# Raw weight loads of a two-layer cross-attention kernel: from SyncE's DMA queue to ScalarE's, and a different lead for the attention steps

## The chip, the cores and the metric

The kernel runs on one core of a Trainium2 chip. A core has five engines that run side by side, each through its own instructions in order: TensorE (PE; its weight loads are listed as PEld), VectorE (DVE), ScalarE (ACT), GpSimd (POOL) and SyncE (SP). Engines wait for each other by semaphores. SP computes nothing here; it issues DMA transfers. The metric is the time of one execution on the device in microseconds (us), smaller is better.

## The reference

Two cross-attention layers run one after the other on `x` (8 batches of 100 rows, 512 wide) with a context `ctx` (8 batches of 722 rows). All is float32.

```python
# layer 0: 16 heads of 32
qn, kn, vn = layer_norm(x), layer_norm(ctx), layer_norm(ctx)
Q, K, V = qn @ wq + bq, kn @ wk + bk, vn @ wv + bv
x1 = x + softmax(Q K^T / sqrt(32)) V @ wo + bo
x2 = x1 + gelu(layer_norm(x1) @ w1 + b1) @ w2 + b2     # 512 -> 2048 -> 512
# layer 1: 8 + 8 heads of 64, no biases
out = softmax((x2 @ Wq) (ctx @ Wk)^T / 8 - 2) (ctx @ Wv) @ Wfc + x2
out = layer_norm(out) * gamma + beta
```

## The kernel before, in words

**Numbers.** Each float32 operand of a matmul is held as two float16 parts, a high and a low one, and most products are three matmuls (`TERMS`: high x high, high x low, low x high). So weights must be scaled and split before use, and this work on the weights is what the change touches.

**Units and heads.** The work is 24 units (`unit_of`): units 0 to 7 are the batches of layer 0, with 16 heads each; units 8 to 23 are the two halves of each batch of layer 1, with 8 heads each. `step(u, h)` (L1465) is the attention of one head: `scores` makes S (PE) and the row maximum `nm` (DVE, 901 ns); in layer 0 `negated` and `negated_T` bring the maximum back into the queries through a small matmul into `nzb` and a copy to `QS` (ACT), and one or two heads later `front0` makes the transposed scores ST (PE), the exponential `p` (ACT), its high part `pt` (ACT) and its low part (POOL). In layer 1 `front1` makes `p` from S, splits it into a `stage` tile (DVE or ACT, then POOL), and a transposing DMA issued by SP fills `pt`. `head_back` multiplies `pt` by V into O (PE). Between the steps, the main loop at the end of the function places pieces of the other work: projections of K and V for the next unit (`pp` and sometimes `nzb` are their PSUM tiles; their results `KN` go through DRAM (`KD`) or directly to `ks`), normalised and transposed context (`prep0`, `prep1`: `nat`, `hl`, `ctxT`), queries (`QN`, `QD`, `QS`), output projections, the feed-forward part (`ffn`, weights by `wst`), and the preparation of weights.

**Preparation of weights.** Layer 0's wq, wk, wv and wo are loaded at the start (`load0`, SP), and are not part of the change. The others (w1, w2, Wq, Wk, Wv, Wfc) are 32 blocks of 512 KB each (`block`, L1057). A block has four stages. `load` (L1061) takes the next of three ring tiles `STG` (named `stage` in the trace, L81) and issues one DMA. `norm` (L1073) squares the block on ACT with a running sum (`hl<-stage`). `scale` adds the sum over partitions with a small matmul (into O or `pp`) and finds a power of two on DVE. `piece` (two for each block) scales and splits half of the block: the high part on ACT (`whl<-stage` or `wres<-stage`), the low part on DVE for one piece, and for the other by an ACT copy (`stage<-stage`) and a subtract on POOL. The result goes to DRAM, from where `wst` tiles fetch it later, or to resident tiles `wres`. The three `stage` tiles are first used for the first context rows, at the start, then by the blocks, and in layer 1 by the attention. `pipeline` (L1045) orders the stages so that loads run ahead of the pieces, as far as three tiles allow.

**What sets the order.** The kernel is written in one program order, and a scheduler then fixes one order of instructions for each engine before the launch. It takes instructions that its model holds to be ready, by their place in the program. Two things bend that. `with tc.high_priority(offset=n)` counts the instructions inside as if they stood n places earlier; `step` uses 105 (80 near the last unit). And `nc.in_order` (L34 to L43, L49) names engines whose instructions keep program order among themselves; `block`'s `load` sets it to `("sync",)` around its DMA, so on SP this load keeps its place among the other loads and start-up transfers that are held so, while an instruction of an engine that isn't named is not held. At the start (L1270 to L1376) almost everything is held in a written order; after that the scheduler is free but for these loads.

Every instruction is recorded by the helper `call` at L40, so the trace gives L40 for all of them; groups are told apart by their tiles.

Of the kernel before, what the change touches and what calls it, by code (L numbers as in the profile page):

```python
# [54 lines left out]
def xattn_kernel(  # L55
# [4 lines left out]
    nc = Core(tc)  # L60
# [49 lines left out]
    def ring(name, tiles):  # L110
        i = counters.get(name, 0)
        counters[name] = i + 1
        return tiles[i % len(tiles)]
# [28 lines left out]
    def small(n=1, dt=F32, tag="sm"):  # L142
        return pool.tile([128, n], dt, tag=f"{tag}{n}", name=f"{tag}{n}", bufs=4)
# [12 lines left out]
    def pow2(*args):  # L156
        for f in pow2_steps(*args):
            f()
# [53 lines left out]
    def colsum(src, n, p=128):  # L212

        ps = psum_misc()
        nc.tensor.matmul(out=ps[:, :n], lhsT=ones[:p, :], rhs=src, start=True, stop=True)
        return ps[:, :n]
# [116 lines left out]
    def split_piece(dst_hi, dst_lo, raw, s, on_pool=False):  # L333
        nc.scalar.activation(dst_hi, raw, AF.Copy, scale=s)
        if on_pool:
            nc.scalar.activation(raw, raw, AF.Copy, scale=s)
            nc.gpsimd.tensor_tensor(dst_lo, raw, dst_hi, ALU.subtract)
            return
        nc.vector.scalar_tensor_tensor(dst_lo, raw, s, dst_hi, ALU.mult, ALU.subtract)
# [30 lines left out]
    def hlt():  # L370
        return ring("hl", HL)
# [324 lines left out]
    def scores(u, h):  # L696
        L, b, hf = unit_of(u)
        S = ps_s.tile([128, 2, 512], F32, tag="S", name="S")
        KS, q = KSt[u, h // 4], QSt[u]
        for j in range(2):  # L700
            sl = slice(j * HALF, (j + 1) * HALF)
            if L == 0:
                nc.tensor.matmul(
                    out=S[:SQ, j, :HALF], lhsT=q[:96, h, :], rhs=KS[:96, h % 4, sl], start=True, stop=True)
            else:
                for t in range(2):
                    nc.tensor.matmul(
                        out=S[:SQ, j, :HALF], lhsT=q[:, t, h, :], rhs=KS[:, h % 4, sl], start=(t == 0), stop=(t == 1))
        nm = small(1, tag="nm")
        nc.vector.tensor_reduce(nm[:SQ], S[:SQ, :, :HALF], AX.XY, ALU.max, negate=True)  # L710
        return S, nm
# [3 lines left out]
    def negated(nm):  # L715
        nz = ring("nm", NM)
        nc.vector.tensor_scalar(nz[:, 96:97], nm[:SQ], 1.0 / MS, None, ALU.mult)
        nc.vector.tensor_scalar(nz[:, 97:98], nz[:, 96:97], -MS, nm[:SQ], ALU.mult, ALU.add)
        return nz

    def negated_T(u, h, nz):
        q = QSt[u]
        z = NZB[:98, h % 4 * 128 : h % 4 * 128 + SQ]
        nc.tensor.matmul(out=z, lhsT=nz, rhs=ident16[:SQ, :SQ], start=True, stop=True)
        nc.scalar.copy(q[96:98, h, :], z[96:98])

    def front0(u, h, nz):
        KS, q = KSt[u, h // 4], QSt[u]
        T = ps_s.tile([128, 2, 512], F32, tag="S", name="ST")
        for c in range(NCH):  # L730
            nc.tensor.matmul(
                out=T[:, c // 3, (c % 3) * SQ : (c % 3) * SQ + SQ], lhsT=KS[:98, h % 4, c * 128 : c * 128 + 128],
                rhs=q[:98, h, :], start=True, stop=True)
        P = ring("p32", P32)[:, : 6 * SQ].rearrange("p (c q) -> p c q", q=SQ)
        nc.scalar.activation(
            P.rearrange("p (a c) q -> p a (c q)", a=2), T[:, :, : 3 * SQ], AF.Exp, scale=sig0)
        pt = ring("pt", PT)
        nc.scalar.copy(pt[:, 0:6, :SQ], P)
        for c in range(0, 6, 3):
            nc.gpsimd.tensor_tensor(  # L740
                pt[:, 6 + c : 6 + c + 3, :SQ], P[:, c : c + 3], pt[:, c : c + 3, :SQ], ALU.subtract)
        return pt

    def front1(u, h, S, nm):
        L, b, hf = unit_of(u)
        if h == 0:
            sums[u] = pool.tile([128, 8], F32, tag="sums", name="sums", bufs=3)
        sg = sig1[:SQ, 2 * hf + h // 4, b : b + 1]
        nb = small(1, tag="nb")
        nc.vector.tensor_tensor(nb[:SQ], nm[:SQ], sg, ALU.mult)  # L750
        P = ring("p32", P32)[:SQ]
        nc.scalar.activation(
            P.rearrange("p (a k) -> p a k", a=2), S[:SQ, :, :HALF], AF.Exp, bias=nb[:SQ], scale=sg,
            accum_out=sums[u][:SQ, h : h + 1])
        p16 = ring("p16", P16)
        if h % 2 == 0:
            nc.vector.tensor_copy(p16[:SQ, 0, :SK], P)
        else:
            nc.scalar.copy(p16[:SQ, 0, :SK], P)
        eng = nc.vector if u == LAST and h >= 4 else nc.gpsimd  # L760
        eng.tensor_tensor(p16[:SQ, 1, :SK], P, p16[:SQ, 0, :SK], ALU.subtract)
        pt = ring("pt", PT)
        nc.sync.dma_start_transpose(pt[:, :, 0:SQP], p16.rearrange("p t k -> p (t k)"))
        return pt
# [69 lines left out]
    LAST = 3 * B - 1  # L834
# [222 lines left out]
    def block(w, kind, i, col, scr=None, dst=None, total=None, done=None):  # L1057

        st = {}

        def load():  # L1061
            raw = ring("raw", STG)
            if kind == "rows":
                st["raw"] = raw.rearrange("p (c n) -> p c n", c=2)
                src = w[i * 256 : (i + 1) * 256, :]
            else:
                st["raw"] = raw.rearrange("p (c n) -> p c n", c=KC)
                src = w[:, i * 256 : (i + 1) * 256]
            nc.in_order = ("sync",)
            nc.sync.dma_start(out=st["raw"], in_=src.rearrange("(c p) n -> p c n", p=128))  # L1070
            nc.in_order = ()

        def norm():  # L1073
            st["u"] = u = small(1, tag="ub")
            nc.scalar.activation(
                hlt(), st["raw"].rearrange("p c n -> p (c n)"), AF.Square, accum_out=u)

        def scale():
            ut = colsum(st["u"], 1)
            t = small(1, tag="ut") if total is None else total[:, i : i + 1]  # L1080
            nc.vector.tensor_copy(t, ut)
            ut = t
            pow2(SC[:, 0, col : col + 1], SC[:, 1, col : col + 1], ut, 7, 1)
            if done is not None:
                done()

        def piece(k):
            raw, s = st["raw"], SC[:, 0, col : col + 1]
            counters["pc"] = counters.get("pc", 0) + 1
            op = counters["pc"] % 2 == 0  # L1090
            half = raw[:, k, :] if kind == "rows" else raw[:, :, k * 128 : (k + 1) * 128]
            if dst is not None:
                w1res[dst] = WRES[dst]
                at = i % 2 * 256 + k * 128
                split_piece(WRES[dst][:, 0, :, at : at + 128], WRES[dst][:, 1, :, at : at + 128], half, s, op)
                return
            o = more.tile([128, 1024], F16, tag="whl", name="whl", bufs=2)
            if kind == "rows":
                split_piece(o[:, :E], o[:, E:], half, s, op)
                nc.sync.dma_start(out=scr[2 * i + k].rearrange("p a b -> p (a b)"), in_=o)  # L1100
            else:
                v = o.rearrange("p (c t n) -> p c t n", c=KC, t=2)
                split_piece(v[:, :, 0, :], v[:, :, 1, :], half, s, op)
                nc.sync.dma_start(out=scr[2 * i + k].rearrange("p a b c -> p (a b c)"), in_=o)
        return dict(load=[(0.1, load)], norm=[(0.8, norm)],
                    scale=[(0.4, scale)], pieces=[(0.8, lambda k=k: piece(k)) for k in range(2)])

# [355 lines left out]
    pending = []  # L1463

    def step(u=None, h=None):  # L1465

        with tc.high_priority(offset=80 if u == LAST or u is None and len(pending) and pending[0][0] >= LAST - 1 else 105):
            new = None
            if u is not None:
                S, nm = scores(u, h)  # L1470
                new = (u, h, S, negated(nm) if u < B else nm)
                if u < B:
                    negated_T(u, h, new[3])
            if len(stages) >= (2 if u is not None and u < B else 1):
                v, g, S_, nm_ = stages.pop(0)
                pending.append((v, g, front0(v, g, nm_) if v < B else front1(v, g, S_, nm_)))
                used.add((v, g))
            if new:
                stages.append(new)
# [84 lines left out]
```

## Time and profile before

| what | value |
|---|---|
| runs shown (median, lowest, highest) | 1545.39, 1542.56, 1549.36 us |
| profiled execution | 1544.16 us |
| its span, first to last instruction | 1542.4 us |
| mean granted TensorE clock | 0.967 |
| DMA moved | 279.20 MB, mean 181 GB/s |
| SP's issues of the 32 blocks | 16 of w1 and w2 from 164.5 to 327.2 us, the last at 616.9 us |
| DMAs issued by ACT | 4, in the first 3 us, 450 to 528 ns each |

How to read it: the page gives each engine's busy time and its share of the span. A line of the waits names the waiting engine and the tile that it was to work on, then who ended the wait, then the total in us, the number of waits and the longest. A line of a group of instructions gives engine, operation, written tile <- read tiles and the count. The granted clock is TensorE's share of its full speed. All later numbers of the profile are from the one profiled execution.

### The profile page before, as it was taken

Reading aid. Unit: us, or ns where it says so; the run is one execution under the profiler, and the core shown is the slowest. Engines: PE = TensorE matmul, PEld = TensorE weight load, DVE = VectorE, ACT = ScalarE, POOL = GpSimd, SP = SyncE. Lnnn points to the kernel's source line nnn. Section 1 sums busy time; section 2 is a strip of 40 time slices with the busy share of each in tenths; the row PEclk is TensorE's granted clock in tenths of the full one; section 3 lists DMA queues with packets and bytes.
Section 4 is the critical chain, followed back from the end, with each engine's and each line's share of the span. In section 5 each row is a group of like instructions: output and inputs, shape, how many; then the busy total and the mean of one; then the engine's idle time right before and its main releaser. Section 6 shows DMA issues by size and latency. Waiting matters only on the chain.

```text
span 1542.4 us, 33741 instructions
## 1 busy us (share of the span) xinstructions
PE 1386.5 (90%) x12586; PEld 983.2 (64%) x12586; DVE 1019.0 (66%) x2761; ACT 813.9 (53%) x1550; POOL 578.1 (37%) x570
## 2 busy tenths in 40 slices
PE   6888888887879999888999899999899999999996
PEld 5666676665657776556666566576566676566674
DVE  7878778879795776575455755456755555646555
ACT  4456667787865776554344343444344544334442
POOL 3245466655564453462122321322322322313341
PEclk9899889999989999999999999999999999999998
DMA  8567898897976556569576879767869868866684
GB/s 218 127 144 191 213 259 219 228 229 200 251 148 179 164 190 194 122 155 205 140 179 188 170 174 213 170 159 192 179 155 217 189 159 192 186 157 159 148 170 110
DMA packets 456636, 279.20 MB, mean 181 GB/s; under 512 B 348932, under 2 KB 387860, under 8 KB 456472
## 3 DMA queue, kind: packets, MB, share of 16 engines
q1 hardware_dynamic: 454328, 277.02, 73.8%
q8 instruction: 99, 1.62, 0.5%
q14 instruction: 65, 0.53, 0.1%
q10 hardware_dynamic: 2112, 0.01, 0.1%
q0 software_dynamic: 32, 0.01, 0.0%
HBM read 150.88 MB, written 35.30 MB: 121 GB/s over the span
## 4 chain that ended last, share of the span: by engine, by line
PE 45%; DMA 12%; DVE 5%; SPq 5%; ACT 3%; issue 3%; POOL 1%; POOLq 0%; ACTq 0%; DVEq 0%
PE pp L40 27%; PE nzb L40 10%; SPq L40 5%; PE S L40 4%; PE O L40 4%; DMA pt<-stage 2%; DMA xs<-X 2%; DMA ks<-KN 2%; DVE nm L40 1%; ACT p L40 1%; DMA stage<-in_L_xattn_Wk_dram 1%; DMA QS<-QD 1%; DMA wst<-WFS 1%; DMA wst<-W1S 1%; DMA ctxT<-hl 1%
## 5 line engine op out<-in xcount | busy, mean ns | idle before, releaser
L40 POOL TENSOR_TENSOR stage<-p,stage 100x722 f16<-100x722 f32 x124 | 194.4, 1572 | 484.2 <-DVE stage L40 254.2
L40 PE MATMUL pp<-ctxT,wres 128*128 128x361 f16 x1836 | 326.8, 327 | 22.4 <-DVE KN L40 5.6
L40 PE MATMUL pp<-wres,ctxT 128*128 128x256 f16 (+3 forms) x2004 | 337.3, 320 | 8.0 <-DVE nm L40 3.0
L40 PEld LDWEIGHTS <-wres 128*128 128x128 f16 x2496 | 241.8, 101 | 151.4 <-issue 32.9
L40 PEld LDWEIGHTS <-ctxT 128*128 128x128 f16 (+1 forms) x2376 | 238.0, 104 | 140.8 <-issue 14.5
L40 DVE TENSOR_REDUCE nm<-S 100x1 f32<-100x722 f32 x256 | 230.0, 901 | 69.1 <-PE S L40 63.7
L40 POOL TENSOR_TENSOR pt<-p,pt 128x300 f16<-128x300 f32 x256 | 200.5, 806 | 178.5 <-ACT pt L40 105.0
L40 PE MATMUL O<-V,pt 128*128 128x64 f16 (+5 forms) x3840 | 200.3, 191 | 19.0 <-DMA pt<-stage 6.5
L40 PEld LDWEIGHTS <-pt 128*128 128x128 f16 (+1 forms) x3840 | 173.1, 99 | 57.4 <-DMA pt<-stage 8.1
L40 PE MATMUL S<-ks,QS 128*100 128x361 f16 (+1 forms) x768 | 175.7, 326 | 29.2 <-DVE nm L40 8.8
L40 ACT ACTIVATE p<-S,nb,sig 100x722 f32<-100x722 f32 x128 | 121.7, 952 | 120.8 <-DVE nb L40 104.3
L40 DVE TENSOR_TENSOR V<-pp,V 128x256 f16<-128x256 f32 (+2 forms) x196 | 90.7, 464 | 108.5 <-ACT V L40 107.9
L40 ACT CAST V<-pp 128x256 f16<-128x256 f32 (+2 forms) x196 | 79.1, 407 | 150.0 <-PE pp L40 105.1
L40 PEld LDWEIGHTS <-QS 128*100 128x100 f16 (+1 forms) x768 | 87.5, 127 | 54.5 <-issue 25.5
L40 ACT ACTIVATE p<-ST,sig 128x600 f32<-128x600 f32 x128 | 97.1, 759 | 27.3 <-PE ST L40 21.2
L40 PEld LDWEIGHTS <-wst 128*128 128x128 f16 x1152 | 99.8, 98 | 13.8 <-issue 4.0
L40 ACT CAST KN<-pp 128x361 f16<-128x361 f32 x89 | 40.9, 460 | 98.0 <-PE pp L40 91.9
L40 ACT CAST pt<-p 128x600 f16<-128x600 f32 x128 | 87.9, 690 | 2.1
L40 PE MATMUL nzb<-ctxT,wres 128*128 128x361 f16 x468 | 82.9, 321 | 2.4 <-DVE sx L40 1.3
L40 DVE TENSOR_TENSOR KN<-pp,KN 128x361 f16<-128x361 f32 x89 | 47.2, 531 | 53.3 <-ACT KN L40 51.6
L40 PE MATMUL nzb<-wres,ctxT 128*128 128x512 f16 (+2 forms) x372 | 80.4, 365 | 0.0
L40 PE MATMUL ST<-QS,ks 98*128 98x100 f16 x768 | 60.0, 210 | 16.5 <-ACT p L40 12.4
(268 smaller groups left out, 2038.7 us busy)
## 6 DMA issues: line engine op xcount, KB each, us to landing
ks<-KN SPq DMA_DIRECT2D x256, 90.2 KB
nat<-in_ctx_dram SPq DMA_DIRECT2D x78, 256.0 KB
ks<-KD SPq DMA_DIRECT2D x96, 180.5 KB
wst<-W1S SPq DMA_DIRECT2D x64, 256.0 KB
wst<-W2S SPq DMA_DIRECT2D x64, 256.0 KB
wst<-WFS SPq DMA_DIRECT2D x48, 256.0 KB
KD<-KN SPq DMA_DIRECT2D x32, 361.0 KB
QS<-QD SPq DMA_DIRECT2D x85, 100.0 KB
```

Source lines behind the costliest of these rows:

```text
L40: r = f(*args, **kwargs)
```

## The change

The DMA of a block's `load` is called on `nc.scalar` instead of `nc.sync`: ACT issues it, in ACT's own DMA queue. `nc.in_order` still names `sync` alone around it, so the load isn't held in program order any more. And the lead of `step` becomes 120 instead of 105; the 80 near the last unit stays.

```diff
             nc.in_order = ("sync",)
-            nc.sync.dma_start(out=st["raw"], in_=src.rearrange("(c p) n -> p c n", p=128))
+            nc.scalar.dma_start(out=st["raw"], in_=src.rearrange("(c p) n -> p c n", p=128))
             nc.in_order = ()
...
-        with tc.high_priority(offset=80 if u == LAST or u is None and len(pending) and pending[0][0] >= LAST - 1 else 105):
+        with tc.high_priority(offset=80 if u == LAST or u is None and len(pending) and pending[0][0] >= LAST - 1 else 120):
```

## The prediction

> **What bounds the kernel now.** I first read the page's busy times and its rows of DMA, then a table of busy time by stage, then what TensorE (PE) waits for, and last the lines of the loads that move.
>
> From the page:
>
> ```profile
> PE 1386.5 (90%) x12586; PEld 983.2 (64%) x12586; DVE 1019.0 (66%) x2761; ACT 813.9 (53%) x1550; POOL 578.1 (37%) x570
> ...
> q1 hardware_dynamic: 454328, 277.02, 73.8%
> ...
> HBM read 150.88 MB, written 35.30 MB: 121 GB/s over the span
> ```
>
> PE is busy for 90% of the span, so a change off PE can win back at most the other 155.9 us. Nearly all data goes through q1, SyncE's queue. By stage (columns: span, busy PE, PEld, DVE, ACT, POOL, then granted clock, DMA share, GB/s):
>
> ```profile
> 160.00:460.00 300.00, 247.76 (x2598) 191.70 (x2596) 249.86 (x812) 225.81 (x419) 173.39 (x198) 0.92 0.87 220
> 460.00:700.00 240.00, 216.36 (x2171) 159.13 (x2170) 157.35 (x415) 151.67 (x278) 114.09 (x128) 0.96 0.60 166
> 700.00:1500.00 800.00, 766.07 (x6427) 509.98 (x6425) 458.82 (x1038) 342.88 (x682) 218.20 (x151) 0.99 0.76 176
> ```
>
> All 32 loads that change lie between 164.5 and 617 us. There PE idles 52.2 + 23.6 us; after 700 us it idles 34 us in 800. In the first row the granted clock is 0.92, which is 24 us of full clock lost in 300; beside 52.2 us idle that is 0.46 us for each idle one. Where PE idles less (third row) the clock is 0.99. I therefore count one us of PE waiting in layer 0 as **1.46 us**. The dips come with idleness, but the trace doesn't show which wait makes which dip, so the factor lies between 1 and about 1.5.
>
> What PE waited for between 160 and 700 us (total, times, longest):
>
> ```profile
> PE ST L40 <- ACT p L40: 11.9, 11, 1.9
> PE pp L40 <- DVE KN L40: 9.2, 9, 3.6
> PE nzb L40 <- ACT QS L40: 7.5, 10, 1.6
> PE S L40 <- DVE nm L40: 5.4, 5, 1.8
> PE O L40 <- ACT hl L40: 4.4, 2, 3.7
> PE nzb L40 <- DVE nm L40: 3.4, 3, 2.0
> PE pp L40 <- DVE nm L40: 3.4, 3, 1.9
> PE S L40 <- ACT p L40: 3.3, 6, 1.6
> PE S L40 <- DMA QS<-QD: 3.2, 1, 3.2
> ```
>
> The attention chain (score, maximum, QS, ST, exp) ends most of it. Transfers end 9.1 us (QS 3.2, yT 2.3, pt 1.4, WOS 1.1, WQS 0.8, ks 0.3). A raw load acts through the block's square on ACT (the row PE O <- ACT hl). The loads on SyncE (min/median/max ns), and who waited for them (us, times):
>
> ```profile
> L40 SPq DMA_DIRECT2D stage<-in_L_xattn_w_dram x16: 383/396/507, 164.5 to 327.2; - x16
> ...
>   ACT hl L40: 12.7, 10
> ```
>
> The worst of those waits, on ACT, in front of the first blocks:
>
> ```profile
> 168.93 1.06 ACT L40 ACTIVATE hl<-stage 128x1024 f16<-128x1024 f32 x1 [2.60 <-DMA stage<-in_L_xattn_w_dram]
> ...
> 172.22 1.06 ACT L40 ACTIVATE hl<-stage 128x1024 f16<-128x1024 f32 x1 [0.65 <-DMA stage<-in_L_xattn_w_dram]
> ```
>
> **The change, part by part.** I compared the orders of the two built programs. The first three loads move from head 21 of layer 0 to ACT's setup, right behind the last readers of the three ring tiles (about 31 us). The other 29 stay within a head or a few of where they were, since a load can't start before the pieces of the block three earlier are done. Negative is a gain; times are PE waiting unless said otherwise.
>
> 1. SyncE loses 32 issues. Their durations sum to 13.4 us of some 260 us that it issues between 160 and 700 us: 5%. What waits behind them are ks, QS, wst and the transposes, whose waits on PE are the 9.1 us above. 5% of 9.1 is **-0.5**. Bounds: -9.1 (all gone) and 0, since the queue loses work and gains none.
>
> 2. The first three loads are early. ACT no longer idles 2.60 + 0.65 us at 169 to 172 us; PE's own gaps behind it there are 0.78, 0.33, 0.31 and 1.17 us on the timeline: **-2.6**. Bounds -4.4 (the whole row PE O <- ACT hl) and 0. If this cover goes, POOL and the attention chain are late next.
>
> 3. Those three loads, 1.57 MB, now run at 31 to 40 us, beside the transposes of ctxT and xT that SyncE issues from 31.5 to 37.7 us; PE waits 3.5 us for ctxT there, on the path. The DMA share is 0.61 and 0.64 in 30 to 40 us and 0.20 in 40 to 45. At 272 GB/s (10 to 20 us) the loads are 5.8 us of all engines, and 30 to 50 us leaves some 9.8 us free, so most is hidden: **+1.5**. Bounds 0 and +8.7 (all of it in front, at the mean 181 GB/s).
>
> 4. ACT gains 32 issues. Three fall into ACT's idle gaps of 1.28 and 1.79 us at 31 and 35 us. The other 29 at 0.42 us are 12.2 us on an engine that runs in order; queued behind each are p, QS, pt and V, which PE waits for. PE's waits for ACT (11.9, 7.5, 4.4, 3.3 and smaller ones, 29.3 us) beside ACT's 377.5 busy us are 0.078 us for each ACT us: **+0.95**. Bounds 0 (all in ACT's idle quarter) and +12.2.
>
> 5. ACT now does the loads' waits. Each load waits for POOL's subtract of the last piece. In the trace it ends 1.2 to 3.2 us, mean 1.6, after the end of ACT's own part of that piece. In the built order the load stands mostly 4 to 7 ACT instructions behind; the fifth instruction started 2.8 us behind in the mean, so only 0.7 us of waiting would have come in 32 blocks. Four stand 2 or 3 behind and may wait about 1 us. In 27 of 32 the load also waits on a DMA semaphore, that of an earlier transfer out of eight in turn; the spacing of SyncE's issues (425 in 540 us, 1.27 us) puts that some 10 us back, and the chain of waits has raw loads of 5.9 to 8.1 us, so it has mostly landed. I take 2 us on ACT, at 0.078: **+0.16**. Bounds 0 and +29 (a whole us at each load, all of it reaching PE).
>
> 6. Steps stand 120 instead of 105 places earlier, 14%. Attention waits in layer 0 (ST, nzb, S, O on p, QS, nm, pt and pb) sum to 41.1 us and projection waits (pp on KN, nm, V, QN) to 17.0; 14% moved from one to the other is -5.9 + 2.4 = -3.5. But in the built order layer 0's score matmuls stand 5.0 matmuls *later* in the mean (0.5 us at 0.095 us each): the preference alone moves them 8.8 earlier, the loads alone 18.2 later. I take a third, **-1.2**; bounds -13.7 (a third of 41.1) and +13.7. In layer 1 O's matmuls stand 11.5 later in the mean, median 0 (1.4 us at 0.119); PE waits 5.0 us for transposed pt there. **-1.5**, no clock factor; bounds -5.0 and +5.0.
>
> Sum: layer 0 -0.5 - 2.6 + 0.95 + 0.16 - 1.2 = -3.2, times 1.46 = -4.7; start +1.5 and layer 1 -1.5 cancel. The profiled execution took 1544.16 us (span 1542.4), 1.2 less than the median of the runs, 1545.39: 1539.5 there, **1541 us** as a median.
>
> **Two rules of the Trainium skill.** The DMA engines' share of 0.87 in 160 to 460 us is the row on which more bandwidth would have to show. "DMA: Bandwidth & Descriptors", section "Issuing engines are not separate DMA queues", says that DMAs of all issuers share the same 16 engines and that spreading them saves sequencer time alone. It speaks against the change: by it only term 1 is left of what a second queue could bring. The clock of 0.92 is the row for the other: "TensorE: Matmul & The Clock Gate", section "HAM oscillation", asks for PE gaps over about 3.4 us before the clock halves. By it the short waits above return no clock, and the sum would be -3.2 us instead of -4.7.
>
> **Rivals.** (a) *Faster by reordering*: the earlier steps do take a third off the attention waits: 13.7 x 1.46 = 20 us, 1525. For it: those are the largest rows. Against it: scores don't stand earlier in the built order. (b) *Slower: ACT becomes late.* Each load holds ACT for 0.42 us plus about 1 us of waiting, 41 us in all, and a third (between 0.078 and 1) reaches PE: 13.7 x 1.46 = 20 us, **1565**. It is slower by over 0.5% once 5.3 us reach PE, or 16 us of ACT lateness. For it: ACT is busy for 75% of 160 to 460 us and runs in order. Against it: the 0.7 us of term 5. (c) *The change does little*: loads are still tied to a ring of three tiles, DMA work is the same: 1545. (d) *The start is delayed*: half of the 8.7 us of term 3, 1549.
>
> **The numbers.** The forecast has 0.45 (its own range 1535 to 1547; 0.17 of it faster by over 0.5%, 0.28 within), (a) 0.17, (b) 0.22, (c) 0.10 within, (d) 0.06 (half slower). 0.5% is 7.7 us, about what a measurement of this kernel can tell from no change. Faster 0.34, same 0.41, slower 0.25. The range 1523 to 1564 reaches across (a) and nearly to (b); the open bounds of terms 5 and 6 make it wide.
>
> **What would show it.** Term 2: no idle time of ACT for the first loads; term 3: PE's wait for ctxT near 36 us longer than 3.5 us; terms 4 and 5: idle time of ACT in front of what follows a load; PE <- ACT rows above 29 us mean (b). Term 6: the attention rows' sum well under 41 us means (a). The forecast is wrong if PE's idle time in 160 to 700 us moves by more than 6 us, or that after 700 us by more than 5.

## The result, and the profile after

| | before | after |
|---|---|---|
| median of 20 runs each, taken side by side | 1544.90 us | 1550.91 us |
| lowest, highest | 1536.91, 1551.9 | 1540.6, 1557.35 |
| span of the profiled execution, mean granted clock | 1542.4 us, 0.967 | 1545.6 us, 0.962 |

The ratio is **1.0035, 95% interval [1.0021, 1.0049]**: 0.35% slower. The forecast was 0.3% faster. The size lies within 0.5%, the sign is the other.

From the page of after:

```profile
PE 1387.4 (90%) x12586; PEld 986.3 (64%) x12586; DVE 1005.8 (65%) x2761; ACT 816.4 (53%) x1550; POOL 581.3 (38%) x570
...
q1 hardware_dynamic: 440504, 260.24, 70.4%
q10 hardware_dynamic: 15936, 16.79, 3.7%
```

The page is nearly that of before. 16.78 MB (32 x 512 KB) went from q1 to q10, ScalarE's queue, and no engine is busier by more than 3.2 us. By stage (columns as before):

```profile
160.00:460.00 300.00, 250.96 (x2643) 196.35 (x2641) 243.26 (x809) 228.43 (x424) 177.54 (x203) 0.91 0.85 217
460.00:700.00 240.00, 213.59 (x2078) 156.04 (x2077) 157.81 (x434) 150.04 (x273) 111.70 (x128) 0.95 0.60 164
700.00:1500.00 800.00, 769.29 (x6500) 513.00 (x6499) 459.08 (x1044) 347.16 (x689) 224.12 (x153) 0.99 0.77 177
```

In 160 to 700 us PE idles 75.5 us, as before (75.9). The sum hides a change inside: the waits of PE in the same 540 us of after are others.

```profile
PE O L40 <- POOL pt L40: 9.2, 14, 1.5
PE nzb L40 <- ACT QS L40: 7.4, 5, 4.3
PE S L40 <- DVE nm L40: 6.0, 8, 2.0
PE S L40 <- ACT p L40: 5.6, 5, 1.7
PE O L40 <- ACT pt L40: 4.8, 8, 1.0
...
PE ST L40 <- ACT p L40: 3.9, 6, 1.4
```

ST <- p fell from 11.9 to 3.9 us, but O now waits 14.0 us for pt (rows of POOL and ACT), where it waited 4.2. That looks like an exchange of one wait for another; the runs below take it apart.

At the start, PE's waits between 25 and 60 us in after, and SyncE's issues there (start, duration):

```profile
PE pp L40 <- DMA ctxT<-hl: 8.0, 1, 8.0
```

```profile
31.88 3.48 SPq L40 DMA_TRANSPOSE ctxT<-hl  x2
35.46 6.07 SPq L40 DMA_TRANSPOSE xT<-hl  x2
47.39 0.35 SPq L40 DMA_DIRECT2D KD<-KN  x1
```

The one wait for ctxT is 8.0 us and was 3.5. The row of the two xT transposes spans 6.07 us, 2.90 before: the first issue took 2.54 us instead of 1.25, and the second had to wait for POOL's part of `hl`, which ended at 40.3 us instead of 36.5. The first KD left at 47.39 us instead of 41.50. The first exponential of the attention starts at 67.8 us, 6.3 later. For the first blocks (instructions of tile hl on ACT, 165 to 176 us, of after) the view now says:

```profile
L40 ACT ACTIVATE hl<-stage x3: 1052/1057/1057, 169.0 to 172.1; 128x1024 f16<-128x1024 f32 x3
...
its engine sat idle before it (us, times) until:
  POOL pt L40: 0.6, 1
  DVE nat L40: 0.2, 1
```

No DMA stands in that list: the 2.60 and 0.65 us of waiting for the first loads are gone.

### The profile page after: what moved, and what is told of

The parts are those of the page before. It is cut to its first block, busy times and chain, and to the rows that moved or that the text cites. A ratio compares the mean times of both kernels' runs of the same rounds, so it can differ in the third digit from the quotient of the medians.

```text
span 1545.6 us, 33702 instructions
## 1 busy us (share of the span) xinstructions
PE 1387.4 (90%) x12586; PEld 986.3 (64%) x12586; DVE 1005.8 (65%) x2761; ACT 816.4 (53%) x1550; POOL 581.3 (38%) x570
## 4 chain that ended last, share of the span: by engine, by line
PE 50%; DMA 16%; DVE 14%; SPq 6%; ACT 6%; issue 5%; POOL 2%; ACTq 0%; POOLq 0%; DVEq 0%
PE pp L40 30%; PE nzb L40 10%; SPq L40 6%; PE S L40 5%; PE O L40 4%; DVE nm L40 3%; DMA nat<-in_ctx_dram 3%; DMA ctxT<-hl 2%; ACT p L40 1%; DMA ks<-KN 1%; DMA wst<-WFS 1%; DMA pt<-stage 1%; DVE rt L40 1%; DVE st L40 1%; DVE KN L40 1%
## 5 line engine op out<-in xcount | busy, mean ns | idle before, releaser
L40 POOL TENSOR_TENSOR stage<-p,stage 100x722 f16<-100x722 f32 x124 | 199.4, 1613 | 465.1 <-DVE stage L40 265.5
L40 PEld LDWEIGHTS <-pt 128*128 128x128 f16 (+1 forms) x3840 | 173.3, 99 | 69.7 <-ACT pt L40 14.2
L40 POOL TENSOR_TENSOR hl<-nat,hl 128x512 f16<-128x512 f32 (+2 forms) x48 | 57.2, 1206 | 49.8 <-ACT hl L40 34.7
```

The costliest lines, as they stand in the source:

```text
L40: r = f(*args, **kwargs)
```

## The experiments

Every ratio is to the kernel before, run on the same chip, with its 95% interval. "On SP" and "on ACT" say who issues the 32 loads.

**Who did it, the loads or the lead?** Four runs: the change with the first three loads back on SP; the kernel before with only those three on ACT; each half of the change alone. The edits (the first two have the same conditional line, in both directions):

```diff
-            nc.scalar.dma_start(out=st["raw"], ...)
+            (nc.sync if counters["raw"] <= 3 else nc.scalar).dma_start(out=st["raw"], ...)   # e1, lead 120
+            (nc.scalar if counters["raw"] <= 3 else nc.sync).dma_start(out=st["raw"], ...)   # e4, lead 105
+            nc.scalar.dma_start(out=st["raw"], ...)                                          # e2, lead 105
+            nc.sync.dma_start(out=st["raw"], ...)                                            # e3, lead 120
```

> The changed kernel, but the first three raw loads are issued by SyncE again, at their old place; the other 29 stay on ScalarE and the lead stays 120. Theory A (the three early loads delay the start): head 0's exponential is back from 67.7 to about 61.5 us, TensorE's wait for ctxT near 36 us back from 8.0 to about 3.5 us, and the time is that of the kernel before, ratio 0.998 to 1.002. Rival B (the 29 issues keep ScalarE late): the start is repaired but the time stays, ratio 1.003 or more. Rival C (the lead of 120 places costs it): also 1.003 or more, with the loss after 160 us.

> The kernel before with one thing of the change: the first three raw loads are issued by ScalarE at the start; the other 29 stay on SyncE, lead 105. Theory A: head 0 at about 67.5 us, the wait for ctxT at about 8 us, ratio 1.003 to 1.005, which is the whole loss. Rivals B and C: the start may be late, but the time is made up later, ratio 0.998 to 1.002.

> All 32 loads on ScalarE, lead 105 as before. Theory A: head 0 at about 67.5 us, ratio 1.002 to 1.006. Rival B: the same ratio, with the loss between 160 and 700 us instead of at the start. Rival C: ratio 0.998 to 1.002. The built order has the score matmuls of layer 0 standing 18.2 matmuls later in the mean than before, which could add up to 2 us.

> Loads on SyncE as before, lead 120. Theory A: start as before (head 0 at about 61.5 us), ratio 0.997 to 1.002. Rival B: the same. Rival C: 1.003 or more. My prediction's own term for the lead was 2.7 us faster, a ratio of 0.998.

| run | ratio | interval | median us |
|---|---|---|---|
| e1, after with the first three on SP | 1.0006 | [0.9989, 1.0023] | 1547.67 |
| e4, before with the first three on ACT | 0.9988 | [0.9966, 1.0010] | 1543.79 |
| e2, loads alone | 1.0114 | [1.0088, 1.0139] | 1564.42 |
| e3, lead alone | 0.9914 | [0.9880, 0.9947] | 1532.56 |

In these builds the change is two effects of opposite sign: +1.14% for the loads, -0.86% for the lead, and their sum, +0.28%, is close to the +0.35% measured. The start alone is not the cause: e4 has the delay of the start (its first exponential is 7.4 us late) and is no slower. e1 by itself would fit theory A: with the start repaired it is 0.29% below after, with intervals that just touch. e4 contradicts A, and e2 and e3 lie outside what all three theories gave for them, so none of the three holds. e3 is faster than both kernels of the case. Where it gains is seen in PE's waits, 160 to 700 us of e3:

```profile
PE nzb L40 <- ACT QS L40: 7.5, 8, 2.4
PE S L40 <- DVE nm L40: 7.2, 9, 2.5
PE O L40 <- POOL pt L40: 4.8, 11, 1.0
...
PE ST L40 <- ACT p L40: 4.5, 6, 2.5
...
PE pp L40 <- DVE KN L40: 3.7, 10, 0.9
```

I added the rows in the two groups of term 6, from the waits of four kernels between 160 and 700 us, and split the spans of the profiled executions at the same places of the work (us):

| | before | e3, lead alone | e2, loads alone | after |
|---|---|---|---|---|
| attention waits (ST, nzb, S, O on p, QS, nm, pt, pb) | 41.1 | 34.7 | 50.4 | 50.3 |
| projection waits (pp on KN, nm, V, QN) | 17.0 | 7.7 | 14.3 | 9.8 |
| up to the first exponential | 61.4 | 61.8 | 68.2 | 67.8 |
| layer 0, heads 0 to 24 | 119.2 | 120.1 | 124.7 | 117.1 |
| heads 24 to 56 | 152.1 | 149.2 | 164.2 | 154.4 |
| head 56 to 128 and four heads of layer 1 | 355.0 | 345.0 | 350.4 | 357.8 |
| the rest | 854.5 | 851.0 | 854.2 | 848.4 |

The lead took 6.4 us of attention waits and 9.3 of projection waits out; the loads brought the attention waits back (+9.3 without the lead, +15.6 with it).

**Do both effects hold at other leads?** Two more leads, 112 and 135, with the loads on SP (s) and on ACT (a); the edit is the number in `step` and, for a, the engine of the DMA.

> Loads on SyncE, lead 112. So far, lead 120 alone gave 0.9914 and the 32 loads on ScalarE alone 1.0114; together 1.0035. Theory D (the lead works by its size: more lead, fewer waits of the attention chain): between 0.992 and 0.999. Theory E (each setting only gives another order, good or bad by chance): anywhere between 0.99 and 1.015, without regard to the neighbours.

> Loads on ScalarE, lead 112. Theory F (the loads on ScalarE cost by themselves, whatever the order): about 0.012 above the run with lead 112 and loads on SyncE, as at 105 (0.0114) and 120 (0.0121). Theory E (order by chance): the difference is unlike these two, and may be below nothing.

> Loads on SyncE, lead 135. Theory D: 0.980 to 0.991, or at least no worse than 0.9914 if the gain is used up. Theory E: anywhere between 0.99 and 1.015.

> Loads on ScalarE, lead 135. Theory F: about 0.012 above the run with lead 135 and loads on SyncE. Theory E: unlike that. In all runs with the first loads on ScalarE I expect head 0's exponential at 67 to 69 us instead of 61 to 62.

| lead | on SP | on ACT | ACT less SP |
|---|---|---|---|
| 105 | 1 (before) | 1.0114 | +1.14% |
| 112 | 1.0015 [0.9985, 1.0045] | 1.0104 [1.0056, 1.0152] | +0.89% |
| 120 | 0.9914 [0.9880, 0.9947] | 1.0035 [1.0021, 1.0049] | +1.21% |
| 135 | 1.0006 [0.9981, 1.0032] | 1.0150 [1.0089, 1.0211] | +1.44% |

The loads on ACT cost at every lead, 1.17% or 18 us in the mean. The lead is no slope: only 120 gains, and its neighbours on both sides are as before. So 120 isn't "more of a good thing" but one order that fits (theory E; the ranges of D were missed by s112 and s135). a135 shows one way in which a load can cost. ACT's timeline there (start, duration, instruction, idle time before and who ended it), then POOL's, then PE's:

```profile
583.49 0.23 ACT L40 CAST QS<-nzb 2x100 f16<-2x100 f32 x1
586.93 0.37 ACTq L40 DMA_DIRECT2D stage<-in_L_xattn_Wk_dram  x1
587.35 0.76 ACT L40 ACTIVATE p<-ST,sig 128x600 f32<-128x600 f32 x1 [3.62 <-POOL whl L40]
```

```profile
584.52 1.26 POOL L40 TENSOR_TENSOR xs<-xs,boB 100x512 f32<-100x512 f32 x1 [4.87 <-DVE nm L40]
585.75 1.15 POOL L40 TENSOR_TENSOR whl<-stage,whl 128x512 f16<-128x512 f32 x1
```

```profile
584.68 0.42 PE L40 MATMUL ST<-QS,ks 98*128 98x100 f16 x6
588.16 0.76 PE L40 MATMUL S<-ks,QS 96*100 96x361 f16 x2 [3.06 <-ACT p L40]
```

ACT is done with QS at 583.72. The next in its order is the load, whose ring tile POOL still reads, until 586.90. Behind the load stands an exponential whose scores PE finished at 585.1. ACT sits 3.62 us, PE 3.06: of this wait 85% reached PE.

**Which loads, and does the held order matter?** e5 is e2 with the first three loads on SP. h1 is the change with the loads held in ACT's program order, which puts the first three behind the start again. u1 has lead 120, loads on SP, but not held. The last two are needed because every kernel above with a load on ACT also released it from the held order.

```diff
+            (nc.sync if counters["raw"] <= 3 else nc.scalar).dma_start(out=st["raw"], ...)   # e5, lead 105
...
+            nc.in_order = ("scalar",)    # h1: ahead of nc.scalar.dma_start, lead 120
...
+            nc.in_order = ()             # u1: ahead of nc.sync.dma_start, lead 120
```

> Lead 105; the first three loads on SyncE, the other 29 on ScalarE. With lead 120 these 29 cost 0.0092 (1.0006 against 0.9914). If that is a cost of their own, 1.007 to 1.012 here; if it is an order met by chance at lead 120, anything from 0.995 to 1.005. Head 0 at 61 to 62 us.

> Lead 120, all 32 loads on ScalarE, but held in program order on it, so that the first three come behind the written start (in the built order at about their old place). The start theory: head 0 at 61 to 62 us again. If the 29 issues on ScalarE cost by themselves: about 1.0006, as e1. Otherwise 0.992.

> Lead 120, all loads on SyncE, but not held in program order; the built order puts the first three right behind the early transfers of the start. The start theory: head 0 late again (65 us or more), since it is the place of the three loads and not their engine that delays the transposes; and without the 29 on ScalarE the total is 0.992 to 0.997. If the engine matters for the start: head 0 at 61 to 62 us.

e5 gave 1.0119 [1.0087, 1.0151], as e2: the 29 later loads cost, the first three don't. h1 repaired the start (first exponential 1.0 us late instead of 6.3, ctxT waited for 3.3 us) and is no faster than after, 1.0044 [1.0020, 1.0068], where e1's 1.0006 was expected. u1 gave 0.9995 [0.9971, 1.0019], above the 0.992 to 0.997 expected: on SP too the loads lose the gain of the lead when they are no longer held, 0.81% against e3 without any load on ACT. Its first exponential is 4.3 us late, but on another wait: ctxT took 3.2 us, QS <- QD 4.1 (1.7 in e3).

In the seven kernels with the later loads on ACT I added, from the traces, ACT's idle time in which a load was issued and that ended right behind the issue (after 60 us, profiled executions; the issue's own time is in it):

| kernel | h1 | after | a112 | e1 | e2 | e5 | a135 |
|---|---|---|---|---|---|---|---|
| held, us | 0.6 | 2.1 | 4.7 | 4.7 | 6.5 | 9.5 | 14.4 |
| ratio | 1.0044 | 1.0035 | 1.0104 | 1.0006 | 1.0114 | 1.0119 | 1.0150 |

Over all seven the ratio rises with the time held (correlation 0.79), but different leads are mixed in it. Within lead 120 (h1, after, e1) it falls, and with each kernel set against the one of its lead with the loads on SP the correlation is 0.39. So the runs don't show that holding makes the cost. In after it can't be most of it: in the two longest holds, of 0.73 and 0.69 us up to 556.4 and 576.8 us, PE had no gap above 0.1 us, nor in the 1.5 us behind the issue. And 9.3 of the 12.5 us of issues ran beside the ACT instruction in front of them. ACT lost 4.7 us in all there, 3.1 to issues and 1.6 idle ahead of them, where the loads cost 1.21%, or 18.7 us.

**The ring's wait or the issue?** Two edits with all loads on SP and held. In w, ACT writes two columns of the ring tile ahead of each load, so that ACT has the wait for the tile and SP the issue. In i and j, ACT issues one more DMA, of 4 bytes, after the first piece of each block: an issue that was meant to bring no new wait. i writes into a new tile of 4 bytes, j into a row of DRAM that is no longer read. p1 has the 29 later loads on GpSimd.

```diff
+            nc.scalar.copy(raw[:, 0:1024:1023], ones[:, 0:2])                 # w1 lead 120, w2 lead 105
...
+    tiny = const.tile([1, 1], F32, name="tiny")                               # i1 lead 105, i2 lead 120
+                if k == 0:
+                    nc.scalar.dma_start(out=tiny, in_=SC[0:1, 0, col : col + 1])
...
+                    nc.scalar.dma_start(out=MSD[0:1, 0:2], in_=SC[0:1, 0, col : col + 1].bitcast(F16))  # j1 105, j2 120
...
+            (nc.sync if counters["raw"] <= 3 else nc.gpsimd).dma_start(out=st["raw"], ...)   # p1, lead 105
```

> Lead 120, SyncE issues all loads at their old place (as in e3, 0.9914), but in front of each load ScalarE copies two columns into the ring tile, so that it has the ring's waits for POOL and DVE in its own order, plus some 0.2 us; the loads overwrite the two columns. Theory G (what the 29 loads cost on ScalarE are the waits, and the order that comes with them): 0.998 to 1.003, near e1's 1.0006. Theory H (the issue in ScalarE's queue costs, by the second queue or the DMA semaphores): 0.990 to 0.994.

> Lead 105, all loads issued by SyncE as before; ScalarE writes two columns of the ring tile ahead of each load, so the waits for the ring tile lie on ScalarE while the issue stays on SyncE. At lead 105 the 29 later loads on ScalarE cost 1.19%. Theory W (the cost is the ring wait in ScalarE's fixed order): 1.006 to 1.012 of the kernel before, that is at least half of 1.19%. Theory I (the cost is the issue on ScalarE, or its queue): 0.998 to 1.002. Theory O (each new order of instructions draws its own time, whatever is changed): anything from 0.992 to 1.012, without relation to the +0.47% of the same edit at lead 120.

> Lead 105, all loads issued by SyncE as before; after the first piece of each block ScalarE issues one more DMA, of 4 bytes from the block's scale, which is there already. So ScalarE issues 32 DMAs that wait for nothing new. Theory I: 1.006 to 1.012. Theory W: 1.000 plus at most 32 issues of 0.4 us times 1/3, 0.3%: 0.999 to 1.003. Theory O: anything from 0.992 to 1.012, without relation to the same edit at lead 120.

> The 32 additional 4-byte DMAs on ScalarE, loads on SyncE, lead 120. The kernel with lead 120 alone stands at 0.9914. Theory I: 0.998 to 1.004 (the 0.9 to 1.2% of the loads come back). Theory W: 0.990 to 0.995. Theory O: anything from 0.988 to 1.006.

> As the run with 32 additional 4-byte DMAs issued by ScalarE at lead 105 (1.0056), with the same order of instructions on every engine, but they go into a DRAM row that is no longer read, so no on-chip tile is added and all tiles keep the addresses of the kernel before. Theory I (issues by ScalarE cost time wherever they write): 1.004 to 1.008. Theory L (the added tile, which moved the other tiles, made the loss; it showed in the last 410 us too, where no such DMA is left): 0.996 to 1.002.

> The same at lead 120; with the added tile it was 1.0117, lead 120 alone 0.9914, and the additional DMAs left ScalarE idle for only 0.3 us. Theory I: 1.006 to 1.014. Theory L: 0.990 to 0.998. Between the two: both have a part.

> Lead 105; the first three loads on SyncE, the other 29 issued by GpSimd, on which the ring wait is partly its own order (most loads wait for GpSimd's own subtract) and which is busy for 37% of the span against ScalarE's 53%. With ScalarE in its place the ratio was 1.0119. Theory W: 0.998 to 1.005, since what is queued behind a waiting load on GpSimd (low parts of pt, splits) is waited for less. Theory I taken as the price of leaving SyncE's queue: 1.008 to 1.015. Theory O: anything from 0.992 to 1.015.

| | lead 105 | lead 120 |
|---|---|---|
| on SP | 1 | 0.9914 |
| w, wait on ACT | 0.9950 [0.9927, 0.9973] | 0.9961 [0.9942, 0.9981] |
| i, issue on ACT, new tile | 1.0056 [1.0035, 1.0077] | 1.0117 [1.0088, 1.0146] |
| j, issue on ACT, no new tile | 0.9977 [0.9955, 1.0000] | 1.0009 [0.9989, 1.0029] |
| p1, 29 loads on GpSimd | 1.0021 [1.0002, 1.0039] | |
| 29 loads on ACT (e5, e1) | 1.0119 | 1.0006 |

Neither half explains the cost by itself. The wait alone gains 0.50% at lead 105 and loses 0.47% at 120. The issue alone (j) gains 0.23% and loses 0.95%. Of the ranges written ahead, w2 and i2 lie outside those of both W and I, i1 just below that of I, w1 between those of G and H, and i2 is also above that of O; j1 fits L, j2 lies between I and L, and p1 fits W. w left ACT idle for only 0.9 and 2.0 us ahead of the copies: the scheduler put the copies where their tile was free, so the long hold of a135 isn't in these kernels, and the full price of the ring's wait was not tried alone. Nor was a fourth ring tile, which would take the wait away. p1 speaks against the loss of SP's queue as the cost, since on GpSimd the loads cost 0.21% where ACT's 29 cost 1.19%; it is a single build.

At lead 120 the issues of i and j waited for next to nothing (ACT idle for 0.1 us ahead of the 32). At lead 105 two of them waited for the scale, which DVE had still to write: 2.2 and 4.3 us in j1. The longer one, on ACT and then on PE:

```profile
339.76 0.22 ACTq L40 DMA_DIRECT2D MSD<-SC  x1
340.02 0.23 ACT L40 CAST QS<-nzb 2x100 f16<-2x100 f32 x1 [4.52 <-DVE SC L40]
```

```profile
339.72 0.27 PE L40 MATMUL pp<-wres,ctxT 128*128 128x256 f16 x1 [0.27 <-DVE SC L40]
```

ACT sits 4.52 us here, longer than in a135, but PE only 0.27, and j1 is no slower than before. So the 85% of a135 is one case and not a rule.

What the small edits show instead is the scatter. Five kernels of lead 120 with the loads on SP (e3, w1, u1, j2, i2) lie between 0.9914 and 1.0117 with a mean of 1.000, and e3 is the lowest of them. Its 0.86% are real for that build, but don't survive small edits. The cost of the loads stands out from the scatter: the twelve kernels with the 29 later loads on SP have a mean of 1.000, the seven with them on ACT lie between 1.0006 and 1.0150 with a mean of 1.008. p1's 1.0021 lies within both groups.

i and j have the same instructions in the same order on every engine; only where the 4 bytes go, and so where later tiles lie, differs. Both times j is faster, by 0.8 and 1.1%. In the issues the two differ (tile views of i2, then of j2; min/median/max ns):

```profile
L40 ACTq DMA_DIRECT2D tiny<-SC x32: 569/570/1181, 176.7 to 662.4; - x32
```

```profile
L40 ACTq DMA_DIRECT2D MSD<-SC x32: 221/222/494, 175.6 to 663.7; - x32
```

But in the profiled executions layer 0, where these issues are, takes the same time (at its end i2 is 1.5 us ahead of j2). The 9.9 us between these two come after it, where ACT issues no DMA. The last part of layer 1, from the same exponential to the end, of i2 and then of j2:

```profile
1146.30:1565.40 419.10, 389.66 (x3443) 263.25 (x3441) 231.14 (x518) 174.28 (x352) 117.52 (x79) 0.99 0.75 165
```

```profile
1143.10:1555.60 412.50, 386.93 (x3443) 262.29 (x3440) 231.42 (x518) 173.99 (x352) 117.43 (x79) 0.99 0.74 167
```

The stage with the same 3443 matmuls takes 6.6 us longer, 2.7 of it busy time of PE; between i1 and j1 it is 4.2 of 7.6 us. These are single executions, and j2's is the slowest of its twelve (1557.32 us, median 1549.14), so they show only a part of the 1.1%. What differs in the programs is where the 4 bytes go and where later tiles lie. The trace shows no addresses: that the place of the tiles makes the difference is a guess.

## Why the prediction was wrong, step by step

The sum was -4.7 us and came out as +5.4 (0.35% of 1544.9). The terms for the loads and for the lead were both far too small, with opposite signs; that the forecast missed by less than either is luck.

- **Terms 4 and 5 failed.** I priced the 29 issues at 12.2 us x 0.078 and the ring's waits at 2 us x 0.078, 1.6 us with the clock. The loads cost 14 to 22 us (0.89 to 1.44% at four leads), and PE's attention waits rose with them by 9.3 us at lead 105 and 15.6 at 120, where I had 1.1. The wrong step is the way to the price: ACT's added time, times the mean share of ACT that reaches PE. In after ACT lost only 4.7 us, less than the 14.2 I had, and the loads cost 18.7 us: no share up to 1 gives that, even with the 1.46. In a135 ACT lost 17.3 us, and there the share was wrong too: two holds of 3.2 us each reached PE with 2.5 and 3.1 us. How most of the cost arises stays open. Orders that fit less well are a candidate: I had seen that the loads alone put the scores 18.2 matmuls later, and only set it against the lead's 8.8.
- **Rival (b)** met the number of the loads by luck: it said 1565, the loads alone took 1564.4. Its 41 us of ACT's lateness did not happen; in e2 ACT lost 15.9 us.
- **Term 6 failed in size, and in one sign.** I took -1.2 us in layer 0 and -1.5 in layer 1 from a built order in which the scores move little; the lead alone gave 13 us in e3. I had the projection waits rise by 2.4 us; they fell by 9.3. Rival (a) came true in part, for that build alone: 1525 forecast, 1532.6 measured, and 6.4 us off the attention waits instead of 13.7. The mean shift of the scores is no measure of the gain: in i2 and j2 they stand 9.0 matmuls earlier than before and in s135 13.8, as early as in e3 (8.9) or earlier, and none of the three gains.
- **Term 3** had the right mechanism and a size too small: ctxT came 4.5 us later, +1.5 forecast, within its bounds of 8.7. By e4 and h1 it cost nothing in the end, which I hadn't foreseen; e1, with the start repaired, is 0.29% below after, so a small part is possible.
- **Term 2** was right in the trace, 3.25 us of ACT's idle time gone, but no run shows a gain from it; e4, which has it alone with term 3, is within its interval of no change.
- **Term 1** can't be told apart: DMA waits of PE in 160 to 700 us were 9.1 us and are 9.4.
- **The signs that I named** were weak. PE's rows of ACT did not rise above 29 us (26.1), though the loads cost time; rows of others rose, such as POOL's pt (3.2 to 9.2). And PE's idle time in 160 to 700 us moved by 0.4 us, where I had said that only more than 6 would refute me: two effects cancelled in it (its waits sum to 74.9 us before, 66.3 with the lead alone, 81.3 with the loads alone, 74.6 in after).

The 1.46 us for each us of waiting was about right or a little low. Head 56 to 128 and the four heads behind, of after and then of e3:

```profile
339.30:697.20 357.90, 311.19 (x3094) 231.29 (x3091) 255.13 (x735) 241.38 (x441) 183.82 (x209) 0.93 0.66 179
```

```profile
331.10:676.10 345.00, 304.13 (x3104) 228.22 (x3102) 252.49 (x732) 240.57 (x440) 180.72 (x210) 0.94 0.69 184
```

After takes 12.9 us longer and idles 5.8 us more (46.7 against 40.9). The mean granted clock is 0.928 and 0.941, so 25.6 and 20.5 us of full clock are lost: 0.55 and 0.50 us beside each idle one, near the 0.46 of the prediction. The longest idle time of PE in this stage of after is 3.3 us, so the clock was below 1 without a longer gap. It was halved seven times there, for 3.4 to 17 us. In the 3.4 us ahead of each PE was busy for 18 to 49%, and ahead of four of the seven no single gap was above 1.5 us. The Trainium skill, "TensorE: Matmul & The Clock Gate", section "HAM oscillation", asks for gaps over about 3.4 us; this stage doesn't agree with it.

In layer 0 a raw load took about as long in either queue: between 160 and 460 us a median of 5.75 us before and 5.87 after, from the issue to the last update of its semaphore. "DMA: Bandwidth & Descriptors", section "Issuing engines are not separate DMA queues", fits this: it says that issuing from several engines saves time on the sequencer and nothing else.

## What to carry to other kernels

Before a DMA goes to an engine that computes, ask what it waits for and what stands behind it in that engine's order. A load that waited for its tile held an exponential in a135, and 3.06 of 3.62 us reached PE; in j1 a hold of 4.52 us reached it with 0.27. No mean share of the engine tells the two apart. When a change has two parts, price and run them apart: here +1.2% and -0.9% looked like a change that does little. And where a scheduler rebuilds the order with each edit, a gain of 1% at a single setting is a property of that build; try its neighbours before you give it a cause.

## What was not expected of the hardware

- 1.57 MB of loads in a second queue, issued at 30.8 to 34.3 us, went with a longer wait of PE for the transposed ctxT: 8.0 us instead of 3.5 in after, 7.7 to 8.8 us in all five kernels profiled with these loads early on ACT, 3.2 to 3.5 us in the five compared without. In after the issue of one xT transpose took 2.54 us instead of 1.25.
- An issue on ACT that has nothing to wait for is all but free to ACT: in j2 6.9 of the 7.4 us of the 32 issues ran beside the instruction before them.
- A 4-byte DMA took ACT 570 ns to issue into an on-chip tile and 222 ns into DRAM; a 512 KB load took 375 ns (medians of i2, j2 and after).
- The same order of instructions, with a 4-byte target in a new tile or in DRAM, differed by about 1% in time; the cause isn't known.
